# Attention vectors of the first graph layer computed beside the features, at the start of a two-layer graph kernel

## The chip, the cores and the metric

The kernel runs on one core of one Trainium2 chip. Its metric is the device time of one launch in microseconds (us). A core has five engines that work side by side, each through its own queue in order: TensorE (PE, matrix products; its weight loads are shown apart as PEld), VectorE (DVE), ScalarE (ACT), GpSimd (POOL), and SyncE (SP), which here only issues loads and stores. Matrix products land in PSUM[...]; everything else is in SBUF.

## The reference, cut to what matters

There are 64 graphs of 256 nodes with 512 features each, all in float32. Two layers follow each other, each with a residual and a layer norm.

```python
# layer 0: graph attention, 8 heads of 64 units
feats  = einsum('bnf,hfu->bhnu', x, W)
e_self = einsum('bhnu,hu->bhn', feats, a_self)      # one logit per node and head
e_neigh= einsum('bhnu,hu->bhn', feats, a_neigh)
dense  = leaky_relu(e_self[..., :, None] + e_neigh[..., None, :], 0.2)
att    = softmax(dense - 1e10 * (1 - adj))
out    = relu(einsum('bhij,bhju->bhiu', att, feats) + b)
x      = layernorm(x + out)
# layer 1: q, k, v of x; softmax(q k^T) * 0.33 + 0.33 * adj + 0.33 * exp(-adj); times v; W_out
x      = layernorm(x + layer1(x, nodemask, adj))
```

The logits need no features: `e_self = x @ (W_h a_self_h)`. The vector `W_h a_self_h`, 512 long for each head, is the "attention vector in x's space"; there are 16 of them, two per head.

## The kernel before, in words

Nodes are tiled in two tiles of 128 (`T = 2`), features in four blocks of 128 (`C = 4`), and heads in two groups of four (`HG = 4`). Graphs run one after the other, overlapped as a pipeline: while graph b is in layer 0, graph b-1 is in the projections of layer 1 and graph b-2 in its attention. The order of all work is written out by hand: each step is a call of `do(stage, graph, step)`, and `in_order` ties every instruction to the one before it on its engine. So the sequence of calls is the sequence of each engine's queue. The main loop (`attention0_beside_projections1`, `attention1_beside_projections0`) serves graphs 2 and later, with fast products of seven instead of eight block multiplications. Graphs 0 and 1 go through `start` and `second_beside_first` with plain products. Only `start` and the helpers that graphs 0 and 1 use are touched.

The steps in `start`, with their names in the profile:

- `xT_rows` (L524): x of graph 0 is turned by TensorE (tile `pt`) and copied to `xT` by ScalarE.
- `turned_weights` (L420, `pw`) turns the layer-0 weights `wf` by products with the identity; `attention_vectors` (L437, `pwa`) multiplies them with the attention coefficients (`a2`, made by GpSimd from `acol`), and VectorE copies the 16 vectors into `wa`.
- `features(t, g)` (L87 through `halved`, tile `pf`): the features of one node tile and one head group, four steps over the feature blocks, each as two half products of 64 columns of weights. `copied` (L673) adds the bias while it moves them from PSUM to `v`.
- `logits` (L663, `pl`): x times `wa`, graph 0 alone. In graph 1 `vectors_placed` (L448) has put the vectors beside the weights, so that the features come with their logits (66 columns per head instead of 64).
- `maxima` (L90 `pr`, L581 to L585): the logits are turned into rows, and the row maximum per head is taken; its second part spreads that maximum over the partitions by a product (L570, `pn`). `columns` (L612 to L620) makes the exponentials per node.
- `factors` (L606, `pg`): the exponentials of the rows, 8 rows, are spread over all partitions by a product with `sel`. 
- `aT`, `far`, `shared`: the adjacency, its exponentials, and the term it gives to layer 1.
- `weights` (L724, `pT`): VectorE makes the unnormalized attention of one head; `scaled` (L681) scales the features on ScalarE; `product` (L747, `av`) multiplies them; `norm0` divides, for graph 0 by VectorE (L768, L770), for the others by ScalarE (L778); `end`, `squares`, `norm` are residual and layer norm.
- `proj1 qk` and `values` (L87, `pq_p`, `pv_p`): layer 1.

`keep_busy` (L211) issues products of zeros that nothing reads, at five places in the start. Before `start`, the code issues the loads in the order of SP's queue: x, the mask, half of the layer-0 weights (the other half goes through ScalarE's queue), the attention coefficients, the bias, the adjacency, x of graph 1 and then all weights of layer 1 (`load_weights1`, L265).

PSUM is shared in two pools: tag `mm` has four tiles of one bank, tag `sc` two tiles of two banks.

Of the kernel before, what the change touches and what calls it, by code (L numbers as in the profile page):

```python
# [17 lines left out]
def kernel(  # L18
# [95 lines left out]

    X, XB, ADJB, MROW = {}, {}, {}, {}
# [33 lines left out]
    load_rows(0)  # L149
    mask_sb = io.tile([NB, N], U8, tag="mask", name="mask_sb", bufs=4)  # L150
    nc.sync.dma_start(mask_sb, nodemask)
    C2, F2 = C // 2, F // 2
# [11 lines left out]
    load_wf(nc.scalar, 0)  # L164
    load_wf(nc.sync, 1)

    acol = small.tile([P, 2, HG], FT, tag="acol", name="acol", bufs=1)
    for k, a in enumerate((a_self, a_neigh)):
        nc.sync.dma_start(acol[:, k, :], a.rearrange("(g r) u -> (r u) g", r=2))
# [3 lines left out]
    a2 = consts.tile([P, HG, 2, 2], FT, name="a2")  # L173
    nc.vector.memset(a2, 0.0)
# [5 lines left out]
    load_adj(0)  # L180
# [4 lines left out]
    wo_sb = consts.tile([P, 7, C2, F2], FT, name="wo_sb")  # L185
# [3 lines left out]
    for r in range(2):  # L189
        rows = slice(r * U, (r + 1) * U)  # L190
        nc.gpsimd.tensor_copy(a2[rows, :, r, :].rearrange("p g s -> p s g"), acol[rows])

    sel = work.tile([H, H + 1, P], FT, tag="rb", name="sel", bufs=1)
    nc.vector.memset(sel[:, H, :], 1.0)
# [13 lines left out]
    def keep_busy(dst, n):  # L208

        for _ in range(n):  # L210
            matmul(dst, idle, idle, start=True, stop=True)  # L211

    keep_busy(ps_tile([P, P], "pi"), 6)
    maskf = work.tile([NB, N], FT, tag="adjT", name="maskf", bufs=1)
    nc.vector.tensor_copy(maskf, mask_sb)
    pm = ps_tile([P, T, NB], "pm")
    for t in range(T):
        transpose(pm[:, t, :], maskf[:, t * P : (t + 1) * P])
    hide = consts.tile([P, T, NB], FT, name="hide")
    nc.vector.tensor_scalar(hide, pm, -1.0, HIDE, op0=ALU.add, op1=ALU.mult)  # L220
    m33 = consts.tile([P, T, NB], FT, name="m33")
    nc.vector.tensor_scalar_mul(m33, pm, L_BOTH)


    maskz = io.tile([NB, N], FT, tag="y", name="maskz", bufs=1)
    nc.vector.transpose(maskz, maskf)
# [188 lines left out]
    def turned_weights(g):  # L415

        pw = ps_tile([P, C, P], f"pw_{g}")
        for c in range(C):
            for r in range(2):
                matmul(  # L420
                    pw[r * U : (r + 1) * U, c, :],
                    wf[c // C2][g // 2][:, c % C2, 2 * (g % 2) + r, :U],
                    ident,
                    start=True,
                    stop=True,
                )
        tag = "both" if g < HG - 1 else "pT"
        wT = WA[g] = work.tile([P, C, P], FT, tag=tag, name=f"wT_{g}", bufs=4)
        nc.scalar.copy(wT, pw)
        in_order()  # L430

    def attention_vectors():

        pwa = ps_tile([P, C, HG, 4], "pwa")
        for g in range(HG):
            for c in range(C):
                matmul(pwa[:, c, g, :], WA[g][:, c, :], a2[:, g], start=True, stop=True)  # L437
        wa = WA["columns"] = work.tile([P, C, H, 2], FT, tag="hC", name="wa", bufs=1)
        nc.vector.tensor_copy(
            wa.rearrange("p c h s -> p (c h s)"), pwa.rearrange("p c g k -> p (c g k)")  # L440
        )
        in_order()

    def vectors_placed():

        for k in range(2):
            for g in range(2):
                nc.vector.tensor_copy(  # L448
                    wf[k][g][:, :, :, U:],
                    WA["columns"][:, k * C2 : (k + 1) * C2, g * HG : (g + 1) * HG],  # L450
                )
        in_order()
# [16 lines left out]
    def proj0(b):  # L469
# [14 lines left out]
        def far():  # L484
            AT[b] = work.tile([P, T, N], FT, tag="at", name=f"at_{b}", bufs=1)
            FAR[0] = work.tile([P, T, N], FT, tag="far", name=f"far_{b}", bufs=1)
            nc.scalar.activation(FAR[0], pa, AF.Exp, scale=-1.0)
            nc.scalar.activation(AT[b], pa, AF.Exp, bias=neg, scale=NEG)
            mrow = small.tile([P, N], FT, tag="mf", name=f"mf_{b}", bufs=1)
            nc.scalar.copy(mrow, MROW[b])  # L490
            FAR[1] = mrow
# [25 lines left out]
        def from_rows():  # L517
            for t in range(T):
                pt = ps_tile([P, C, P], f"pt_{b}_{t}")
                if t == 0:  # L520
                    keep_busy(pt[:, 0, :], 4)
# [40 lines left out]

        def maxima(part=None):

            if part == 1:
                pn = ps_tile([P, P], f"pn_{b}")
                if b == 0:
                    keep_busy(pn, 3)
                ROW["max"] = pn[:, :H]
                matmul(ROW["max"], sel[:, H, :], ROW["diag"], start=True, stop=True)  # L570
                return
            ps = ps_tile([P, 2, N], f"pr_{b}")
            if b == 0:
                keep_busy(ps[:, 0, :P], 3)
            ps = ps[:H]
            for s in range(2):
                for t in range(T):
                    transpose(ps[:, s, t * P : (t + 1) * P], V0[b][:, t, :, U + s])
            grow = small.tile([H, N + 1], FT, tag="grow", name=f"grow_{b}", bufs=1)
            nb = small.tile([H, 1], FT, tag="nb", name=f"nb_{b}", bufs=2)  # L580
            nc.vector.tensor_reduce(grow[:, N : N + 1], ps[:, 1, :], AX.X, ALU.max)  # L581
            nc.vector.tensor_scalar_mul(nb, grow[:, N : N + 1], -0.8)
            nc.scalar.activation(grow[:, :N], ps[:, 0, :], AF.Exp, bias=nb, scale=-0.8)
# [4 lines left out]
        def factors(part=None):  # L588
# [7 lines left out]
            h = HG if part == 1 else 0  # L596
            while h < (HG if part == 0 else H):
                n = 2 if b == 0 and h < HG else HG
                if n == 2:
                    pg = ps_tile([P, n, N], f"pg_{b}_{h}")  # L600
                else:
                    pg = psum.tile([P, n, N], FT, tag="sc", name=f"pg_{b}_{h}", bufs=2)
                if b == 0 and h == 0:
                    keep_busy(pg[:, 0, :P], 3)
                for k in range(n):
                    matmul(pg[:, k, :], sel[:, h + k, :], grow[:, :N], start=True, stop=True)  # L606
                    GB[b].append(pg[:, k, :])
                h += n

        def columns():  # L610
            nd = small.tile([P, T, H], FT, tag="nd", name=f"nd_{b}", bufs=2)
            nc.vector.tensor_sub(  # L612
                nd,
                V0[b][:, :, :, U + 1],
# [29 lines left out]
        def features(t, g):  # L644

            pf = PF[t, g] = ps_tile([P, HG, UX], f"pf_{b}_{t}_{g}")
            for c in range(C):
                halved(
                    pf[:, :, :cols],
                    xT[:, c, t * P : (t + 1) * P],  # L650
                    wf[c // C2][g][:, c % C2, :, :cols],
                    start=(c == 0),
# [3 lines left out]
        cols = U if b == 0 else UX  # L656

        def logits():

            pl = ps_tile([P, T, H, 2], f"pl_{b}")  # L660
            for t in range(T):
                for c in range(C):
                    matmul(  # L663
                        pl[:, t],
                        xT[:, c, t * P : (t + 1) * P],
                        WA["columns"][:, c],
                        start=(c == 0),
                        stop=(c == C - 1),
                    )
# [969 lines left out]
```

## Time and profile before

| | us |
|---|---|
| median of 3 runs | 2838.47 |
| lowest and highest | 2838.01, 2840.29 |
| the profiled execution | 2838.85 |
| its span | 2837.1 |
| first product of layer 1 (`pq_p`), graph 0, starts | 57.37 |
| first value product of layer 1 (`pv_p`), graph 0, starts | 77.46 |

The span is what the hardware profiler saw of one execution; the profiled execution's own time is 1.75 us longer. In the profile, a group line gives the source line, engine, operation, output and inputs with their shape (partitions x elements), the count, the busy time and the mean of one. A wait line gives who waited for whom, how long in sum, how often, and the longest. In a line of busy time by stage come the stretch, its length, then the busy time of each engine with its count, the TensorE clock that the chip granted (1.00 is full speed), the share of the DMA engines, and the rate. Products are pipelined, so the mean of one is longer than the pitch between two.

### The profile page before, as it was taken

Reading aid. Unit: us, or ns where it says so; the run is one execution under the profiler, and the core shown is the slowest. Engines: PE = TensorE matmul, PEld = TensorE weight load, DVE = VectorE, ACT = ScalarE, POOL = GpSimd, SP = SyncE. Lnnn points to the kernel's source line nnn. Section 1 sums busy time; section 2 is a strip of 40 time slices with the busy share of each in tenths; the row PEclk is TensorE's granted clock in tenths of the full one; section 3 lists DMA queues with packets and bytes.
Section 4 is the critical chain, followed back from the end, with each engine's and each line's share of the span. In section 5 each row is a group of like instructions: output and inputs, shape, how many; then the busy total and the mean of one; then the engine's idle time right before and its main releaser. Section 6 shows DMA issues by size and latency. Waiting matters only on the chain.

```text
span 2837.1 us, 93579 instructions
## 1 busy us (share of the span) xinstructions
PE 2813.9 (99%) x39172; PEld 2231.9 (79%) x39172; DVE 2556.9 (90%) x5135; ACT 1805.0 (64%) x5033; POOL 252.6 (9%) x528
## 2 busy tenths in 40 slices
PE   9999999999999999999999999999999999999998
PEld 7787787787787887887877888878778778788775
DVE  4999999999999999999999999999999999999984
ACT  3556666666666666666666666666666666666663
POOL 0000001000100100000010001001001000100011
PEclk9999999999999999999999999999999999999999
DMA  6445445554455454454454544554554544545532
GB/s 125 105 119 141 118 136 133 127 139 122 132 144 122 125 143 122 128 138 121 137 127 131 140 122 132 144 121 125 137 126 131 141 118 137 133 127 139 122 113 72
DMA packets 774508, 362.84 MB, mean 128 GB/s; under 512 B 690396, under 2 KB 692428, under 8 KB 758088
## 3 DMA queue, kind: packets, MB, share of 16 engines
q1 hardware_dynamic: 771976, 356.33, 48.5%
q8 instruction: 311, 5.10, 0.8%
q14 instruction: 109, 0.89, 0.1%
q10 hardware_dynamic: 2112, 0.52, 0.1%
HBM read 288.37 MB, written 68.13 MB: 126 GB/s over the span
## 4 chain that ended last, share of the span: by engine, by line
PE 97%; DVE 1%; DMA 1%; ACT 1%; issue 0%; POOL 0%; SPq 0%; DVEq 0%; POOLq 0%; ACTq 0%
PE pq_p L87 27%; PE po_p L87 14%; PE pf_p L87 13%; PE pv_p L87 13%; PE av L747 8%; PE pz L918 8%; PE av L1047 7%; PE pd L957 2%; PE pr L531 1%; PE pf L87 1%; PE po L87 0%; DMA x<-in_x_dram 0%; PE pg L606 0%; DMA mask_sb<-in_nodemask_dram 0%; PE pwa L437 0%
## 5 line engine op out<-in xcount | busy, mean ns | idle before, releaser
L87 PE MATMUL pq_p<-hC,wqk_sb 128*64 128x128 f32 x8192 | 469.7, 273 | 1.1 <-ACT qk L340 1.1
L87 PEld LDWEIGHTS pq_p<-hC,wqk_sb 128*64 128x64 f32 x8192 | 448.6, 137 | 2.3 <-ACT qk L340 1.5
L724 DVE SCALAR_TENSOR_TENSOR pT<-gb,ccol,at 128x256 f32<-128x256 f32 x992 | 403.4, 481 | 17.2 <-ACT ccol L619 17.2
L87 PE MATMUL pq_p<-hT,wqk_sb 128*64 128x128 f32 x6144 | 357.7, 273 | 0.4 <-ACT hT L880 0.4
L87 PEld LDWEIGHTS pq_p<-hT,wqk_sb 128*64 128x64 f32 x6144 | 342.0, 137 | 10.1 <-issue 0.7
L937 ACT ACTIVATE p<-pz,hide 128x512 f32<-128x512 f32 x638 | 333.3, 629 | 8.1 <-PE pz L918 1.0
L1028 DVE TENSOR_TENSOR p<-p,rb 128x1024 f32<-128x1024 f32 x252 | 299.2, 1208 | 3.6 <-DMA rb<-rs 3.6
L1037 DVE TENSOR_TENSOR p<-p,ct 128x1024 f32<-128x1024 f32 x252 | 299.5, 1209 | 0.2
L778 ACT ACTIVATE x<-av,rec 128x64 f32<-128x64 f32 x1008 | 220.3, 335 | 63.5 <-DVE rec L760 63.5
L747 PE MATMUL av<-v,pT 128*64 128x65 f32 x8192 | 253.1, 222 | 3.6 <-DVE pT L724 1.9
L681 ACT ACTIVATE v<-v 128x64 f32<-128x64 f32 x1024 | 251.3, 336 | 6.0 <-DVE v L673 6.0
L87 PE MATMUL pf_p<-wf_sb,xC 128*64 128x264 f32 x1984 | 253.6, 386 | 0.1
L747 PEld LDWEIGHTS av<-v,pT 128*64 128x64 f32 x8192 | 249.4, 138 | 5.3 <-issue 4.7
L87 PE MATMUL pv_p<-wv_sb,hC 128*64 128x256 f32 x2048 | 244.1, 379 | 2.5 <-ACT v L340 2.5
L340 ACT COPY qk<-pq_p 128x512 f32<-128x512 f32 x256 | 149.0, 582 | 153.4 <-PE pq_p L87 149.9
L1047 PE MATMUL av<-p,v 128*64 128x256 f32 x2016 | 240.0, 379 | 2.1 <-DVE p L1037 2.1
L918 PE MATMUL pz<-qk 64*128 64x256 f32 x2048 | 238.6, 383 | 0.0
L340 ACT COPY v<-pv_p 128x256 f32<-128x256 f32 x256 | 95.7, 374 | 221.4 <-PE pv_p L87 221.4
L87 PE MATMUL po_p<-wo_sb,oC 128*64 128x256 f32 x1984 | 235.2, 379 | 0.0
L394 POOL TENSOR_SCALAR rstd_l<-rstd_l 128x2 f32<-128x2 f32 (+1 forms) x130 | 96.2, 740 | 1532.5 <-ACT junk L383 1532.5
L918 PEld LDWEIGHTS pz<-qk 64*128 64x128 f32 x2048 | 192.6, 186 | 44.7 <-issue 24.6
L949 DVE SCALAR_TENSOR_TENSOR both<-p 128x512 f32<-128x512 f32 x256 | 172.4, 675 | 46.5 <-ACT p L937 46.2
(178 smaller groups left out, 4461.7 us busy)
## 6 DMA issues: line engine op xcount, KB each, us to landing
rb<-rs SPq DMA_DIRECT2D x63, 1024.0 KB
gb<-gs SPq DMA_DIRECT2D x62, 1028.0 KB
x<-in_x_dram SPq DMA_DIRECT2D x64, 512.0 KB
hs<-x SPq DMA_DIRECT2D x64, 512.0 KB
xb<-in_x_dram SPq DMA_DIRECT2D x252, 128.0 KB
y<-hs SPq DMA_DIRECT2D x63, 512.0 KB
out_dram<-y SPq DMA_DIRECT2D x63, 512.0 KB
hb<-hs SPq DMA_DIRECT2D x248, 128.0 KB
```

The lines of the kernel that those rows point to most:

```text
L87: matmul(dst[cols], lhsT[:, cols], rhs, **flags)
L340: nc.scalar.copy(out[COPIES[p]], dst)
L681: nc.scalar.activation(V0[b][:, t, h, :U], V0[b][:, t, h, :U], AF.Copy, scale=V0[b][:, t, h, U : U + 1],)
L724: nc.vector.scalar_tensor_tensor(pT[h][:, j, :], GB[b][h], CCOL[b][:, j, h : h + 1], AT[b][:, j, :], op0=ALU.max, op1=ALU.mult,)
L747: matmul(av[r * half : (r + 1) * half, k, :], pT[h][:, j, i : i + half], V0[b][:, j, h, :UA], start=(j == 0), stop=(j == T - 1),)
L778: nc.scalar.activation(X1[b][:, t, h * U : (h + 1) * U], av[:, k, :U], AF.Copy, scale=REC0[g][:, t, k : k + 1],)
L918: matmul(pz[r][:, j, :], QK[b][rows, g, 1, j * P : (j + 1) * P], QK[b][rows, g, 0, :], start=True, stop=True,)
L937: nc.scalar.activation(to, of, AF.Exp, bias=hide[:, j, b : b + 1], scale=U**-0.5,)
L949: nc.vector.scalar_tensor_tensor(both[g], p[:, :, 0, :], TINY, p[:, :, 1, :], op0=ALU.add, op1=ALU.add)
L1028: nc.vector.tensor_mul(p, p, REC[b][:, k : k + 2, g // 2, :] .unsqueeze(2) .to_broadcast([P, 2, T, N]),)
L1037: nc.vector.tensor_add(p, p, CT[b].unsqueeze(1).to_broadcast([P, 2, T, N]))
L1047: matmul(av[0][r * U : (r + 1) * U, g % 2, :], V1[b][:, j, 2 * g + r, :], PROBS[b][g][:, r, j, :], start=(j == 0), stop=(j == T - 1),)
```

## The change: what it does, and the diff

The attention vectors are no longer made by TensorE. Three one-row loads put the attention coefficients and the bias into one partition (`arow`, in space of `wo_sb` that is free then), ahead of everything else on SP's queue. A product with one row of ones spreads the coefficients over all partitions. VectorE (from PSUM) and GpSimd (from a copy that ScalarE makes) multiply them with the weights as they were loaded, and VectorE sums over the 64 units of each head.

The logits of graphs 0 and 1 come straight from x: once as rows (the vectors as weights, 40 columns of which 16 are used and the two kinds start at 0 and 32), once as columns for the neighbours' logits. The transposes of logits are gone, and graph 1's features have 64 columns per head again. The bias becomes the first product of each feature group, one row of ones times the bias row, and the scaling reads the features from PSUM, so that `copied` is gone. The mask's small steps go to ScalarE and behind the first features, graph 0's division goes to ScalarE, `vectors_placed` too. All fillers but four at the very start go. The layer-1 weights are loaded after the adjacency of graph 1, and the calls in `start` have a new order. The row broadcasts are all in two tiles of the `sc` pool.

```diff
+    wo_sb = consts.tile([P, 7, C2, F2], FT, name="wo_sb")
+    arow = wo_sb[0:1, 4:].rearrange("p k c f -> p k (c f)")
+    for k, a in enumerate((a_self, a_neigh, b0)):
+        nc.sync.dma_start(arow[:, k, :], a.rearrange("h u -> (h u)").unsqueeze(0))
+    X[0] = io.tile([P, T, F], FT, tag="hb", name="x_0", bufs=1)
+    for t in range(T):
+        nc.sync.dma_start(X[0][:, t, :], x[0, t * P : (t + 1) * P, :])
...
+    def masks(step):
+        if step == 0:
...
+            nc.scalar.copy(maskf, mask_sb)
+            nc.vector.transpose(maskz, maskf)
...
+        else:
+            pm = MASK.pop("pm")
+            nc.scalar.activation(hide, pm, AF.Copy, bias=-HIDE, scale=HIDE)
+            nc.scalar.mul(m33, pm, L_BOTH)
...
-    def turned_weights(g):
...
+    def attention_vectors(g):
+        if g == 0:
+            WA["psum"] = psum.tile([P, 2, 2, HG, U], FT, tag="sc", name="pa_bc", bufs=2)
+            WA["sbuf"] = io.tile([P, 2, 2, HG, U], FT, tag="x1", name="a_bc", bufs=1)
+            WA["columns"] = work.tile([P, C, 2, B], FT, tag="hC", name="wa", bufs=1)
+            nc.vector.memset(WA["columns"], 0.0)
+            for _ in range(4):
+                matmul(WA["psum"][:, 0, 0, :2], idle, idle, start=True, stop=True)
+        for k in range(2):
...
+            matmul(
+                WA["psum"][:, g, k].rearrange("p h u -> p (h u)"),
+                sel[0:1, H, :],
+                arow[:, k, cols],
...
+        nc.scalar.copy(WA["sbuf"][:, g], WA["psum"][:, g])
...
+    def logit_weights(g, c, step):
+        if step == 0:
...
+            engine, src = (nc.gpsimd, "sbuf") if c % 2 or g and c else (nc.vector, "psum")
+            engine.tensor_mul(
+                prod,
+                wf[c // C2][g][:, c % C2, :, :U].unsqueeze(1).to_broadcast([P, 2, HG, U]),
+                WA[src][:, g],
+            )
+        else:
+            nc.vector.tensor_reduce(
+                WA["columns"][:, c, :, g * HG : (g + 1) * HG], WA.pop((g, c)), AX.X, ALU.add
+            )
...
+        def logits():
+            pl = ps_tile([P, 2, N], f"pl_{b}")
+            for c in range(C):
+                matmul(
+                    pl[: B + H, 0],
+                    WA["columns"][:, c].rearrange("p s k -> p (s k)")[:, : B + H],
+                    xT[:, c],
...
+            near = pl[:, 1, : T * H].rearrange("p (t h) -> p t h", h=H)
+            for t in range(T):
+                for c in range(C):
+                    matmul(
+                        near[:, t],
+                        xT[:, c, t * P : (t + 1) * P],
+                        WA["columns"][:, c, 1, :H],
...
+        def features(t, g, c=None):
+            if c is None or c == 0:
+                PF[t, g] = ps_tile([P, HG, U], f"pf_{b}_{t}_{g}")
                 halved(
+                    PF[t, g],
+                    sel[0:1, H, :],
+                    arow[:, 2, g * HG * U : (g + 1) * HG * U],
+                    start=True,
+                    stop=False,
+                )
...
         def scaled(h):
             for t in range(T):
...
+                v = V0[b][:, t, h]
+                src = v[:, :U] if b > 1 else PF[t, h // HG][:, h % HG]
+                nc.scalar.activation(v[:, :U], src, AF.Copy, scale=v[:, U : U + 1])
```

The new order in `start`, up to the first product of layer 1:

```diff
+        attention_vectors(0)
+        attention_vectors(1)
+        for step in ((0, 0, 0), (0, 1, 0), (0, 3, 0), (0, 0, 1), (0, 2, 0), (0, 1, 1), (0, 2, 1), (0, 3, 1),
+                     (1, 1, 0), (1, 2, 0), (1, 0, 0), (1, 0, 1), (1, 1, 1), (1, 3, 0), (1, 2, 1), (1, 3, 1)):
+            logit_weights(*step)
         do("proj0", 0, "xT_rows")
+        # features of graph 0, group 0: for c in range(C), for t in range(T)
+        masks(0)
+        masks(1)
         do("proj0", 0, "logits")
+        # features (0, 1), blocks 0 and 1
         do("proj0", 0, "maxima")
         do("proj0", 0, "aT")
+        do("proj0", 0, "far", 0)
         load_adj(1)
+        combine_weights1 = load_weights1()
         do("proj0", 0, "maxima", 1)
+        # features (0, 1), blocks 2 and 3
         do("proj0", 0, "columns")
+        # factors 0, factors 1, features (1, 1)
+        # for h in 0..3: scaled, weights; then far 1; products (0, 0), (0, 1) of graph 0
         do("turned", 1, "xT")
         load(2)
+        do("attend0", 0, "rec0", 0)
+        # scaled h 4..7; norm0 (0, 0), (0, 1); weights 4, 5
+        do("proj0", 1, "logits")
         vectors_placed()
+        # graph 1: maxima; graph 0: weights 6, 7
+        # graph 1: features (0, 0), (1, 0), maxima 1; graph 0: products (1, 0), (1, 1)
+        # graph 1: columns, aT, far 0, factors 0, with graph 0's shared 0 behind columns
+        # graph 0: rec0 1, norm0 (1, t), end, squares; graph 1: features (0, 1), (1, 1), factors 1, scaled 0..3
+        # graph 0: norm, from_rows 0 and 1, blocks; load_rows(1); graph 1: weights 0..3
         do("proj1", 0, "qk", "p1")
```

After that, `combine_weights1`, `hC` and the other products of q and k follow as before, with `shared 1` of graph 0 and `far 1` of graph 1 after the product p6, and heads 4 to 7 of graph 1 after p7. The comments in this second part stand for the calls they name.

## The prediction

> **What bounds the kernel now.** I read the page first (shares, then the slices), then the waits of TensorE, then the busy time by stage, and last the groups by form of the first 77.5 us.
>
> ```profile
> PE 2813.9 (99%) x39172; PEld 2231.9 (79%) x39172; DVE 2556.9 (90%) x5135; ACT 1805.0 (64%) x5033; POOL 252.6 (9%) x528
> ```
>
> TensorE is busy 99% of the span, so only TensorE work, its waits or its clock can move the end. Of its named waits in the whole span, 16 us in sum, some 40% lie in the first 58 us; the two largest there:
>
> ```profile
> PE pm L90 <- DVE maskf L215: 2.6, 1, 2.6
> ...
> PE av L747 <- DVE pT L724: 1.9, 1, 1.9
> ```
>
> The columns of the next view, busy time by stage, are TensorE busy, weight loads, VectorE, ScalarE, GpSimd, granted clock, DMA share, GB/s:
>
> ```profile
> 12.70:19.50 6.80, 6.80 (x87) 5.96 (x83) 0.00 (x0) 2.27 (x4) 0.00 (x0) 1.00 0.67 102
> 19.50:29.70 10.20, 9.88 (x47) 8.36 (x48) 2.06 (x7) 0.46 (x1) 0.00 (x0) 0.50 1.35 225
> 29.70:36.60 6.90, 6.90 (x42) 5.26 (x40) 3.38 (x10) 3.67 (x13) 0.00 (x0) 0.99 1.03 153
> 36.60:40.00 3.40, 3.40 (x18) 1.96 (x16) 0.70 (x3) 0.00 (x0) 0.00 (x0) 0.50 0.00 0
> ...
> 57.40:77.50 20.10, 20.10 (x368) 18.72 (x370) 18.44 (x35) 8.36 (x27) 0.00 (x0) 1.00 0.40 104
> 77.50:2837.00 2759.50, 2743.02 (x38360) 2171.54 (x38354) 2516.66 (x5030) 1781.44 (x4970) 248.28 (x512) 1.00 0.49 128
> ```
>
> "Busy" hides something: in 19.5 to 29.7 and 36.6 to 40 us TensorE ran at half clock. Before 12.7 us there is no clock record and the 1.00 shown is empty; the durations say half clock there too: a 128x128 transpose of x took 421 ns at 8.8 to 10.3 us and 272 ns at 55.5. After 77.5 us (first value product of graph 0, 77.46) TensorE is full and that code is unchanged. So the change is worth what it moves that point.
>
> [...] the half-clock stretches are 10.24 and 3.41 us, three windows and one. [...] The window 33.2 to 36.6 was full of the row broadcasts pg (8 rows of weights) and the clock fell; 16.1 to 19.5 held 0.9 us of features and then pwa (4 columns) and it fell; 43.4 to 46.8 held 1.5 us of dense products and it stayed. So products with few rows or few columns count as idle, and about 1.2 to 1.5 us dense per window is the limit.
>
> **The change, part by part.** Prices are from these groups (busy us, mean ns):
>
> ```profile
> L606 PE MATMUL pg<-grow,sel 8*128 8x256 f32 x32 | 7.7, 384 | 0.0
> L437 PE MATMUL pwa<-a,wT 128*128 128x4 f32 x32 | 4.7, 284 | 0.0
> L420 PE MATMUL pw<-ident,wf_sb 128*64 128x128 f32 x48 | 4.2, 332 | 0.0
> L663 PE MATMUL pl<-wa,xT 128*128 128x16 f32 x16 | 3.6, 375 | 0.3 <-DVE wa L439 0.3
> ```
>
> An fp32 matmul is two such instructions. By their pitch in order of time: pg 3.65 us for 8 matmuls, 0.456 each; pwa 4.66 for 16, 0.29; a feature step (two halves, 256 columns) 1.73/4 = 0.43; all double, or nearly, at half clock.
>
> Removed from TensorE: turning the weights (pw) 4.63, pwa 4.66, graph 0's logits 3.60 at half clock, row transposes 0.85 and 0.8, and fillers 1.47 + 0.87 + 0.86 = 3.2 (those ahead of 9 us filled waiting time). Added: row logits, 4 matmuls of 40x256 at 0.43 = 1.7, and column logits, 8 at 0.29 = 2.35, in both graphs, 8.1; eight one-row bias products at 0.43 = 3.5, less 0.2 for graph 1's narrower features. Net 17.7 - 11.4 = 6.3 us less.
>
> Moved off TensorE: the vectors. Eight products of 128x512 and eight reductions. VectorE's 128x512 product takes 0.69 us (the add into qk); the reduction is not shown at this size, 0.41 us for 256 elements, so 0.5 to 0.8, I take 0.65. GpSimd at 128x512 is in no row; its 128x128 select took 0.29[...].
>
> Landing: first, three one-row loads, 0.45 us of issue each, ahead of x on SP's queue: x starts at 2.2 instead of 0.73, and the first data came 1.35 us after the issue. x needs about 2.7 us of the DMA engines and goes ahead of the 256-byte runs of the weights, which finish near 10.7. One-row products for the broadcast: 4 at half clock, 3.3 to 6.7 us. Products from 7.2; GpSimd's five run 8.0 to 9.3, 9.8 (fourth block) to 11.1, 12.4, 13.7, 15.0; last reduction 15.7. TensorE meanwhile: transposes 6.7 to 8.4, ten feature steps 8.4 to 14.9 (half clock until about 12.7), masks 0.3. So the vectors cost TensorE 0.5 us; the cover is graph 0's first features.
>
> Then with full clock, in order: logits 4.1 to 19.8; three steps 1.3; the maximum waits for ScalarE and VectorE (0.4) and takes 0.4; two steps 0.86; pg 3.65 to 26.4; features 2.16; products 2.0; logits 4.1 to 34.6; features 4.3; maximum 0.4; products 2.0; pg 1.9; features 4.3; pg 1.9; turning h 1.05; copy 0.5: the first q/k product at 51.0 (before: 57.37, with 3.84 of pg still to come). From there seven products 12.55 (16.4 less those 3.84 in the trace), 1.4 lost (below) and 3.75 of av: the value product at 68.7 instead of 77.46. That is 8.8 us, with full clock.
>
> The 1.4: behind the add of tile 11 VectorE has wqk 1.22, graph 0's shared 1.55, four heads of weights 3.2, wqk 1.22, add 0.69, in all 8.6 with the add itself, and TensorE has four products, 7.2, before p3 needs the last add.
>
> New waits in the order of the queues: TensorE's logits on the last reduction (all later TensorE work stands behind, 0.5 us as above); VectorE's reciprocal of graph 0 on the first products, with two heads of weights behind it, and its row maximum of graph 1 on graph 1's logits, with two more heads behind. These heads are used by the second products at 39, and VectorE has done them by 37: 2 us of cover, beyond that TensorE waits.
>
> Edits at nothing: masks to ScalarE (needed late), normalization of graph 0 to ScalarE (16 x 0.22, while TensorE does logits and features), scaling straight from PSUM (holds four of the four small banks until columns; the next tile comes after that), vectors placed by ScalarE. The layer-1 weights' sixteen loads (15.2 us of issue, 15.5 to 30.7 now) go behind graph 1's adjacency, which waits for VectorE's turn at about 21: issue to 40, data to 42. Behind them on SP is x of graph 2, needed at 78. First user is VectorE at 46 or later: hidden by 4 us at least; a further delay beyond that would be paid one for one.
>
> **The clock.** Between 15 and 26.4 there are only 1.7 us of dense steps; the fillers that stood there are gone. pg of graph 0 (3.65 plus a bias) must empty a window: one at half clock, 1.7 us lost. The two logits groups (2.8 us of thin work each, 4.5 if 40 columns count as thin) empty one more between them, or two, by the window's phase. I take two windows, 3.4 us, less the 0.4 of the maximum's wait, which a slower TensorE swallows: 8.8 - 3.0 = 5.8. Against the profiled execution's 2838.85 that is 2833.0; the median is 0.4 lower: about 2832.6.
>
> **Rivals.** *The clock eats it*: three or four windows half clocked (logits 0, pg 0, logits 1, pg 1). For: 40 columns and one row may count as idle, and no filler is left. Against: the before has four such windows too. Gain 8.8 - 5.2 to 6.8 = 2 to 3.6: about 2835.5. *The clock holds* (0 or 1 window): gain 7 to 9, about 2830.5. For: graph 1's features come in two blocks of 4.3 between thin groups. *GpSimd late*, the other side: five products in series, so each 0.1 us more on one moves the logits by 0.5. Lost are 5.8 us of forecast when the series is 5.8 longer, at 2.5 us a product; at 3 us, with a window emptied by the wait, 2842. For: never run here at this size[...].
>
> **How the numbers follow.** Forecast (two windows, 2831 to 2834.5) 0.50; clock eats it 0.22; clock holds 0.18; GpSimd late 0.10. Faster by over 0.2% means under 2832.8, the least a measurement of this kernel can tell from none: 0.30 of the forecast's half, all of "holds" and little else, 0.49. Slower by over 0.2% (above 2844.1) 0.06, the rest of "late" and all else 0.45. The range runs from 2828.5 (clock held, 10 us) to 2839.5 (GpSimd at 2.6 us).
>
> **What would show it.** Right: wa's last reduction by 16 us; the first q/k product at 52 to 57; the value product at 70 to 75; two half-clock stretches of one window between 19 and 45. Wrong: TensorE waiting for a reduction over 1 us; a clock at 0.50 for over 10 us; a wait for wqk's load; a wait in graph 0's first products for pT.

## The result, and the profile after

The kernel with the change takes 2844.22 us (median of 14 runs, 2838.32 to 2847.14), the kernel before on the same chip 2839.23 us (14 runs, 2836.55 to 2841.23): a ratio of 1.0017, 95% interval 1.0009 to 1.0026. So it is 5 us slower where 5.8 us of gain were forecast, outside the range of 2828.5 to 2839.5. The profiled execution took 2843.23 us, its span 2841.4.

The page's busy shares don't say why. TensorE has 62 instructions fewer and is busy 9.2 us longer:

```profile
PE 2823.1 (99%) x39110; PEld 2241.4 (79%) x39110; DVE 2559.0 (90%) x5125; ACT 1807.5 (64%) x5054; POOL 254.3 (9%) x531
```

The waits of TensorE up to 300 us. The two of before (2.6 for the mask, 1.9 for the attention of graph 0) are gone, and no new one is over 1.2 us:

```profile
PE pa_bc L420 <- DVE rowmask L177: 1.2, 1, 1.2
PE pq_p L87 <- ACT qk L337: 0.7, 1, 0.7
PE pa_bc L423 <- ACT a_bc L430: 0.7, 1, 0.7
```

Fewer instructions, fewer waits, more time: that leaves the clock, or new products that each take longer; the experiments decide between them. Busy time by stage (columns as before), cut at the edges of the clock records, the first of which is at 17.36 us (the 1.00 shown ahead of it is empty: a 128x128 transpose of x took 428 ns at 7.9 to 9.8 us and 279 in graph 1's, at 62.75):

```profile
17.40:24.20 6.80, 6.75 (x50) 4.14 (x46) 1.48 (x5) 1.33 (x4) 0.00 (x0) 1.00 0.16 23
24.20:37.80 13.60, 13.60 (x46) 8.31 (x47) 4.74 (x11) 3.41 (x14) 0.00 (x0) 0.50 0.83 161
37.80:44.70 6.90, 6.90 (x100) 5.22 (x98) 2.82 (x9) 4.16 (x20) 0.00 (x0) 0.99 1.04 192
44.70:51.50 6.80, 6.80 (x32) 2.99 (x28) 1.34 (x5) 0.01 (x1) 0.00 (x0) 0.50 0.44 69
51.50:64.08 12.58, 12.34 (x133) 8.40 (x131) 8.96 (x20) 7.97 (x27) 2.33 (x8) 1.00 0.13 42
64.08:81.70 17.62, 16.45 (x352) 15.96 (x354) 13.00 (x25) 5.44 (x16) 0.00 (x0) 1.00 0.48 114
81.70:2740.00 2658.30, 2657.22 (x37328) 2122.36 (x37326) 2458.86 (x4928) 1734.87 (x4860) 233.76 (x485) 1.00 0.50 130
```

A window is 3.41 us here: every stretch of the clock record but the last is a whole number of them (6.83 is two, 13.65 four). That a window's work goes with the clock of the next is the prediction's reading, and the window shares below bear it out. The half-clock stretches are four windows and two, where before had three and one. The first value product of layer 1 starts at 81.70 instead of 77.52 us, 4.2 later (77.46, given above for the kernel before, is the start of its weight load), and the span is 4.3 longer: in these two executions the whole loss lies ahead of that product. In order of time, what TensorE did around the late rise of the clock (17.36) and its first fall (24.18):

```profile
9.82 1.12 PE L87 MATMUL pf<-wo_sb,sel 1*64 1x256 f32 x4
10.87 1.12 PE L87 MATMUL pf<-wf_sb,xT 128*64 128x256 f32 x4
11.92 1.12 PE L87 MATMUL pf<-wo_sb,sel 1*64 1x256 f32 x4
12.97 5.39 PE L87 MATMUL pf<-wf_sb,xT 128*64 128x256 f32 x28
...
20.41 1.95 PE L585 MATMUL pl<-wa,xT 128*128 128x8 f32 x16
22.29 0.65 PE L87 MATMUL pf<-wo_sb,sel 1*64 1x256 f32 x4
22.87 1.08 PE L87 MATMUL pf<-wf,xT 128*64 128x256 f32 x8
...
26.29 7.19 PE L622 MATMUL pg<-grow,sel 8*128 8x256 f32 x16
```

The same 16 instructions of the row broadcasts `pg`, 7.19 us here, took about half in the kernel before:

```profile
32.68 3.72 PE L606 MATMUL pg<-grow,sel 8*128 8x256 f32 x16
```

And the groups by form that took the place of `pw`, `pwa` and graph 0's 16-column `pl` (busy us, mean ns, up to 82 us), first TensorE, then GpSimd:

```profile
L622 PE MATMUL pg<-grow,sel 8*128 8x256 f32 x32 | 11.2, 513 | 0.0
...
L87 PE MATMUL pf<-wo_sb,sel 1*64 1x256 f32 x32 | 7.1, 528 | 0.0
...
L585 PE MATMUL pl<-wa,xT 128*128 128x8 f32 x32 | 3.9, 257 | 0.0
L575 PE MATMUL pl<-xT,wa 128*40 128x256 f32 x16 | 3.8, 381 | 0.0
```

```profile
L440 POOL TENSOR_TENSOR prod<-wf_sb,a_bc 128x512 f32<-128x512 f32 x4 | 4.7, 1178 | 4.7 <-ACT a_bc L430 4.7
L440 POOL TENSOR_TENSOR prod<-wf,a_bc 128x512 f32<-128x512 f32 x1 | 1.2, 1187 | 1.9 <-DVE wa L446 1.9
```

GpSimd's product takes 1.18 us where the forecast has 1.3, the author's estimate that no trace of the kernel before shows, and the last reduction ends at 15.5 us (forecast 15.7). The bias line (`pf<-wo_sb,sel`) has one row of weights (1*64): 32 instructions, 7.1 us of busy time.

### The profile page after: what moved, and what is told of

The parts are those of the page before. It is cut to its first block, busy times and chain, and to the rows that moved or that the text cites. A ratio compares the mean times of both kernels' runs of the same rounds, so it can differ in the third digit from the quotient of the medians.

```text
span 2841.4 us, 93467 instructions
## 1 busy us (share of the span) xinstructions
PE 2823.1 (99%) x39110; PEld 2241.4 (79%) x39110; DVE 2559.0 (90%) x5125; ACT 1807.5 (64%) x5054; POOL 254.3 (9%) x531
## 4 chain that ended last, share of the span: by engine, by line
PE 98%; DVE 1%; ACT 1%; issue 0%; POOL 0%; POOLq 0%; DVEq 0%; ACTq 0%
PE pq_p L87 27%; PE po_p L87 14%; PE pf_p L87 14%; PE pv_p L87 13%; PE av L748 8%; PE pz L909 8%; PE av L1038 7%; PE pd L948 2%; PE pf L87 1%; PE pr L539 1%; PE po L87 0%; PE pg L622 0%; DVE p L1019 0%; PE pa_bc L423 0%; PE pl L585 0%
## 5 line engine op out<-in xcount | busy, mean ns | idle before, releaser
L688 ACT ACTIVATE v<-v 128x64 f32<-128x64 f32 x992 | 243.0, 336 | 0.0
```

What stands on the lines that cost most here:

```text
L688: nc.scalar.activation(v[:, :U], src, AF.Copy, scale=v[:, U : U + 1])
```

## The experiments

Two words are used from here on. A product is *full height* when its weights have all 128 rows, and *thin* when they have few rows (1 or 8) or when it streams few columns (4 to 16).

**The theory**: the time is the clock, and the bias products (one row) and the row broadcasts (8 rows) are what empties its windows. **The rivals**: the new products simply cost more time; or what was lost is the fillers that the change removed. The lever: a product over all 128 rows, of which all but the real ones are zero, gives the same sums and, as the runs below show for `pg` (16 instructions in 3.72 us over 8 rows and over 128), takes as long, but is full height.

In brief; each ratio is to the kernel before, run again beside it. "Half" are the half-clock windows between the first clock record and the first value product. They and the value product are those of one profiled execution, the medians those of 5 to 21:

| kernel | half | value product, us | median, us | ratio (95%) |
|---|---|---|---|---|
| before | 4 | 77.5 | 2839.23 | |
| the change | 6 | 81.7 | 2844.22 | 1.0017 (1.0009 to 1.0026) |
| both over 128 rows | 0 | 69.1 | 2831.28 | 0.9972 (0.9961 to 0.9984) |
| only `pg` over 128 | 3 | 75.8 | 2837.59 | 0.9994 (0.9986 to 1.0002) |
| only bias over 128 | 1 | 70.9 | 2833.59 | 0.9981 (0.9974 to 0.9988) |
| twelve fillers | 2 | 78.7 | 2849.55 | 1.0038 (1.0024 to 1.0051) |
| both over 32 | 5 | 80.0 | 2843.22 | 1.0016 (1.0009 to 1.0022) |
| both over 64 | 5 | 80.4 | 2842.59 | 1.0011 (1.0004 to 1.0017) |
| both over 128, no bias | 2 | 69.2 | 2828.48 | 0.9967 (0.9954 to 0.9979) |
| all one-row work over 128 | 0 | 65.0 | 2828.04 | 0.9962 (0.9950 to 0.9975) |
| before, `pg` over 128, late start | 3 | 82.5 | 2842.78 | 1.0018 (1.0011 to 1.0025) |
| before, no later fillers | 5 | 77.0 | 2839.04 | 1.0002 (0.9994 to 1.0010) |
| before, `pg` over 128 | 2 | 74.1 | 2837.07 | 0.9995 (0.9986 to 1.0003) |
| bias 128, `pg` 64 | 0 | 68.2 | 2832.22 | 0.9975 (0.9965 to 0.9985) |
| bias 128, `pg` 32 | 1 | 70.8 | 2833.78 | 0.9982 (0.9975 to 0.9989) |

### Bias and row broadcasts over all rows, together and one by one

The edit (the second and third kernel have one half of it each):

```diff
+    tall = work.tile([P, H + 1, P], FT, tag="rb", name="sel", bufs=1)
+    sel = tall[:H]
+    nc.gpsimd.memset(tall[:, :H], 0.0)
...
+    first = rowmask[:, 0, P // B : 2 * P // B].rearrange("p i b -> p (i b)")
+    nc.vector.memset(first, 0.0)
+    nc.vector.memset(first[0:1], 1.0)
...
+            wide = small.tile([P, N + 1], FT, tag="grow", name=f"grow_{b}", bufs=1)
+            nc.gpsimd.memset(wide[:, :N], 1.0)
+            grow = wide[:H]
...
-                        pg[:, k, :], sel[:, g * HG + k, :], grow[:, :N], start=True, stop=True
+                        pg[:, k, :], tall[:, g * HG + k, :], ROW["wide"][:, :N], start=True, stop=True
...
-                    sel[0:1, H, :],
-                    arow[:, 2, g * HG * U : (g + 1) * HG * U],
+                    first,
+                    brow[:, g * HG * U : (g + 1) * HG * U],
```

(`brow` is 128 rows of zeros with the bias in the first. With it, the bias is loaded behind x and no longer ahead of it. That brought no head start: VectorE writes more zeros first, and TensorE begins at 1.71 us, in the change at 1.17.)

> The changed kernel, with the row broadcasts (8 rows) and the bias products (1 row) made over all 128 rows: the added rows of weights are zero, so the result and the time of each product at a given clock are the same. Clock theory (products over few rows count as idle in the window that sets the TensorE clock, and six half-clock windows cost the forecast gain): the clock rises by 14 us, at most one half-clock window is left in 20 to 52 us, the first value product of layer 1 comes at about 70 to 73 us instead of 81.65, the time is 8 to 11 us under the changed kernel's, about 2834. Work theory (the 11.4 us of added TensorE work simply cost more than was removed, whatever the clock): the same time as the changed kernel, within 1.5 us, 2844.

> The changed kernel with only the row broadcasts over 128 rows. Clock theory: the half-clock stretch at 24 to 38 us shrinks to one or two windows, graph 1's stays; 4 to 6 us under the changed kernel, about 2839. Work theory: 2844.

> The changed kernel with only the bias products over 128 rows. Clock theory: the clock rises one window earlier at the start, graph 1 loses at most one window instead of two, the stretch over the row broadcasts stays; 3 to 6 us under the changed kernel, about 2840. Work theory: 2844.

Measured: 2831.28, 2837.59 and 2833.59 us. In the first, the stretch from the first clock record to the first q/k product, and two lines of its work in order of time:

```profile
14.30:51.50 37.20, 36.77 (x366) 26.38 (x362) 21.45 (x53) 16.91 (x64) 2.84 (x10) 1.00 0.74 137
```

```profile
20.72 0.65 PE L87 MATMUL pf<-wo_sb,rowmask 128*64 128x256 f32 x4
...
23.75 3.72 PE L633 MATMUL pg<-grow,sel 128*128 128x256 f32 x16
```

37.2 us without a break in the clock; `pg` is back at 3.72 us with 16 times the rows. The value product comes 12.6 us earlier than in the change, and the median is 12.9 lower than the change's, more than the 8 to 11 expected. So the clock explains the loss of 5 us and nearly all of the gain that didn't come. That the new products "cost too much" falls as the cause; they are all still there. About 0.7 of the 12.6 us isn't the clock: at full clock a group of bias products takes 0.43 to 0.48 us over 128 rows and took 0.58 over one. Alone, the bias over 128 rows lifts the clock 3.2 us earlier (14.2 instead of 17.4 us) and leaves one window, just behind `pg`:

```profile
23.72 3.72 PE L628 MATMUL pg<-grow,sel 8*128 8x256 f32 x16
...
27.88 1.93 PE L87 MATMUL pf<-wf,xT 128*64 128x256 f32 x8
29.58 1.85 PE L87 MATMUL pf<-wf_sb,xT 128*64 128x256 f32 x8
```

`pg` itself is fast (3.72 us), what follows takes nearly double (eight feature instructions 1.93 us, 1.03 in the first experiment): here the thin window was paid for by the next one. `pg` over 128 rows alone leaves three windows. So the one-row bias is the larger part; the two gains, 10.6 and 6.6 us by the medians, overlap and don't add. A part of the second may be chance: its clock rises at 15.91 instead of 17.36 us though nothing ahead of `pg` differs on TensorE, which is worth 0.7 us in the profiled execution.

### Fillers put back

```diff
+                if (b, t, g) in ((0, 0, 1), (1, 0, 0)):
+                    keep_busy(PF[t, g][:, :2], 3)
...
+                if (b, g) in ((0, 0), (0, 1)):
+                    keep_busy(pg[:, 0, :P], 3)
```

> The changed kernel with fillers back: three products of zeros each ahead of graph 0's second feature group, of each of its two row broadcasts, and of graph 1's first feature group (12 products, 3.5 us at full clock). Clock theory: they cost 3.5 us and save two to four half-clock windows of 1.7 us each: 0 to 4 us under the changed kernel, about 2842. Work theory: 3.5 us more, 2847.7.

Measured 2849.55 us, a miss: slower than the change, though the profiled execution has only two half-clock windows in the start and its value product 3.0 us earlier. Busy time at half clock in the start, and the last 100 us, of this kernel:

```profile
31.70:38.50 6.80, 6.80 (x61) 4.22 (x62) 1.85 (x3) 1.54 (x7) 0.00 (x0) 0.52 1.29 220
...
2740.00:2844.20 104.20, 87.86 (x998) 63.07 (x994) 57.04 (x98) 46.06 (x109) 10.38 (x25) 0.93 0.24 78
```

In the last 100 us, where the last graphs run out and TensorE waits, the clock was 0.93 on average; in the change it was 0.96. That code is the same in both. Over the whole run the mean clock is 0.995 to 0.996 in all five executions, no better than the change's 0.994 to 0.997. So the fillers' own 3.4 us came on top of a clock that was not better in sum. As a cure they fall; since they do take the windows in the start from six to two, their loss is not excluded as a part of the cause. At an equal mean clock of 0.996 this kernel is 4.4 us above the change (2848.2 against 2843.8). Where the profiled execution lost its lead can be read: at 2771.8 us it is still 4.0 us ahead of the change, and the last 72 us cost it 6.8, among them one wait of TensorE for VectorE's `both`, 2.6 us long, where the change has none. Why its end had two half-clock windows more than the change's is not settled.

### How many rows count: 32 and 64

The edit is that of the first experiment with `tall[:32]`, `first[:32]` and so on, then with 64.

> As the version with both kinds of products over all 128 rows, but over 32 rows. If the clock counts a product by its rows (the clock theory as I hold it), 32 of 128 is little more than 8 and the half-clock windows are back: first value product at 77 to 82 us, time 2840 to 2845. If it counts any product of 32 rows or more as work, it stays near the version over all rows, 69 us and 2831. The work theory, which fell with that version, would have no difference between the three.

> The same over 64 rows. Counting by rows: half of the work counts, so one or two half-clock windows, first value product at 70 to 75 us, 2832 to 2837. Counting any product of 32 rows or more: 69 us, 2831.

Measured 2843.22 and 2842.59 us, little better than the change; the second is a miss. Of 64 rows:

```profile
26.77 7.19 PE L633 MATMUL pg<-grow,sel 64*128 64x256 f32 x16
```

At half clock 64 rows did not lift the clock, though two whole windows (27.76 to 34.58 us) were full of 64-row products. But with 64 rows a window from 51.65 to 55.07 us held the clock with only 30% of its time in full-height work and the rest in `pg` and bias of 64 rows, where windows of the other kernels with 28 to 33% of it and thin work for the rest had fallen. That spoke for the share (64 rows count half), with a limit that is harder to reach at half clock. The last two runs below test it.

### Without the bias, and the version that beats both

The first experiment without its eight bias products (the bias of layer 0 is not added for graphs 0 and 1); and the first experiment with everything of one row over 128 rows, the broadcasts of the attention coefficients too, in a tile of its own for each head group:

```diff
-            WA["psum"] = psum.tile([P, 2, 2, HG, U], FT, tag="sc", name="pa_bc", bufs=2)
+        pa_bc = WA["psum", g] = psum.tile([P, 2, HG, U], FT, tag="sc", name=f"pa_bc_{g}", bufs=2)
...
-            for _ in range(4):
+            for _ in range(5):
...
-                sel[0:1, H, :],
+                first,
```

> The version over all 128 rows with the eight bias products left out (the bias of layer 0 is not added for graphs 0 and 1). At full clock these cost 8 x 0.43 = 3.5 us: first value product at 65.5 to 67.5 us instead of 69.1 (some of it may go into waits of VectorE and for the weights' vectors), time about 2828.5. If their price lay in the clock alone: no change, 69 us, 2831.

> The version over all 128 rows, with the broadcast of the attention coefficients over 128 rows too, and in a PSUM tile of its own for each head group, so that VectorE's first product doesn't wait for ScalarE's second copy. Clock theory: the clock rises one or two windows earlier, before 11.5 us, the first features end at 14 to 15 us instead of 16.7, the last reduction is done at 13 to 14.5: first value product at 66 to 68 us, 2829. If the start is bound by the arrival of the weights: no change, 69 us, 2831.

Measured 2828.48 and 2828.04 us. Leaving the bias out saves 2.8 us by the medians, though the ratios' intervals overlap. Its six runs are of two kinds: four at a mean clock of 0.999 take 2827.8 us on average, 3.6 less than the first experiment at that clock (2831.4), as priced, and two at 0.997 take 2832.8. The profiled execution is one of these two, so its value product, 69.2, missed the 65.5 to 67.5 expected. In it the full-height bias is missed: the window 17.75 to 21.16 us, with 40% of its time in such work, let the clock fall.

```profile
17.75:21.16 3.41, 3.24 (x26) 2.35 (x24) 1.11 (x4) 0.43 (x1) 0.00 (x0) 1.00 0.26 31
21.16:27.99 6.83, 6.37 (x19) 4.46 (x20) 0.78 (x5) 3.86 (x15) 0.00 (x0) 0.50 0.42 79
```

The other beats both kernels: 10.4 us under the kernel before, with the value product at 65.0, earlier than expected. Its clock is full from 6.82 us on, up to the first q/k product and beyond:

```profile
4.00 3.29 PE L433 MATMUL pa_bc<-wo_sb,rowmask 128*128 128x256 f32 x8
7.13 1.04 PE L90 MATMUL pt<-ident,x 128*128 128x128 f32 x8
```

```profile
7.06:47.30 40.24, 39.86 (x392) 28.58 (x389) 26.01 (x61) 18.70 (x68) 8.22 (x15) 1.00 0.75 143
```

The 0.7 us that TensorE had waited for ScalarE's copy between the two broadcasts is gone too (the eight instructions run on from 4.00 us without a gap), now that the copy no longer shares a tile with them. The two edits were made together; what each is worth was not measured.

### The same edit, and the fillers, in the kernel before

> The kernel before, with one edit: its row broadcasts pg run over all 128 rows, of which 120 of the weights are zero. If the rule (few rows count as idle) carries over: no stretch at 0.50 at 36.6 to 40.0 us, the pg of graph 0 still at full clock, the first value product at 75.4 to 76.2 instead of 77.46, the median 1.2 to 2 us under the kernel before (2836.5 to 2837.2, ratio 0.9993 to 0.9996). If rows have nothing to do with it: the stretch stays and the ratio is 1.0000.

> The kernel before without the nine zero products ahead of pr, pn and pg of graph 0, which took 3.2 us. If they count as work and hold the clock: the window from 26.3 no longer lifts it, TensorE stays at 0.50 from 19.5 until past pg, and the first value product comes at 77.5 to 82 in spite of 3.2 us less work; the median is 0 to 4 us above the kernel before. If they bought nothing: the value product at 74.3 and the median 2 to 3 us below.

> The kernel before with row broadcasts over all 128 rows, as in the run before this one, but the zeros are written by VectorE ahead of the mask's copy, not by GpSimd behind its wait for the attention coefficients, so that TensorE's first products are not 6.7 us late. If few rows count as idle here too: no stretch at 0.50 after pg of graph 0, first value product at 75.4 to 76.4 (77.46 in the kernel before), median 0.5 to 2 us under the kernel before, the rest up to the windows of the last 100 us. If the 1.7 us that the previous run won back between pg and the first av came from its late start and not from the rows: the stretch is back and the ratio is 1.0000.

In the first of the three the zeros were put in a bad place: they, 0.95 us of GpSimd's time, stood behind GpSimd's copy of the attention coefficients, which waits for their load. VectorE's writes to the same tile waited, and the mask's copy behind them:

```profile
13.25 0.44 PE L90 MATMUL pm<-ident,maskf 64*128 64x64 f32 x2 [9.28 <-DVE maskf L217]
```

TensorE started 6.7 us late, and the kernel is 4.7 us slower. Even so the stretch behind `pg` was gone: the first `av` is 4.93 us later than before's (46.45 against 41.52), so 1.8 of the 6.7 were won back there. With the zeros written by VectorE in time:

```profile
22.20:29.10 6.90, 6.90 (x32) 4.34 (x31) 1.83 (x6) 0.47 (x1) 0.00 (x0) 0.51 1.22 217
29.10:54.00 24.90, 22.19 (x272) 17.66 (x270) 17.21 (x51) 9.95 (x30) 3.62 (x9) 1.00 0.49 89
```

Two windows instead of four, the value product 3.4 us earlier (74.1, ahead of the 75.4 to 76.4 expected; the windows lay better ahead of `pg` as well), and the median 1.0 us lower, with an interval that takes in no change. In the profiled execution 1.8 us are lost again in the last 45 us. The mechanism carries over; its worth in time is at the limit of what these runs tell.

Without the nine later fillers the kernel before has one half-clock window more, and the value product comes at 77.0 us: 3.2 us of work saved, all but 0.5 lost again. The median doesn't move (1.0002). The forecast of 77.5 to 82 was nearly right: they bought about what they cost.

### What a window counts

Every window up to 66 us of thirteen kernels was then read in this way: the time of each product, times its rows over 128; products that stream 16 columns or fewer are left out; the sum divided by 3.41 us. The clock of the next window follows from it with one limit for each state. At full clock the lowest share that held was 0.41, the highest that fell 0.40; at half clock the lowest that rose was 0.86, the highest that did not 0.85. Half clock does about half the work in the same time (`pg` 7.19 us for 3.72), so the two limits are nearly one: 0.40 to 0.41 of the work that a window holds at full clock, and half of 0.85 to 0.86, that is 0.42 to 0.43; some 1.4 us of it. They don't meet exactly, and each rests on two windows. This was read off the traces, so it was tried on two new kernels, the first experiment with `pg` over 64 and over 32 rows:

> The bias over 128 rows, so the clock rises at 14.2 us as in the first experiment, and the row broadcasts pg over 64 rows, at full clock when they begin near 23.7. Share rule (a product counts by its share of 128 rows; a window at full clock holds with 41% or more): the worst window is pg alone, 50 to 56%, so the clock stays at 1.00, pg of graph 0 takes 3.7 us, first value product at 69.0 to 69.5, median 0 to 1 us from the first experiment's (2830.5 to 2832.5). Rule of nothing (64 rows count as idle): one window at 0.50 near 27.8 to 31.2, value product at 70.9, as with 8 rows.

> The same with pg over 32 rows. Share rule: the window 24.4 to 27.8 holds 13% dense work and 87% of pg at a quarter, 35% in sum, under 41%: one window at 0.50 near 27.8 to 31.2, value product at 70.6 to 71.0, median 2832.5 to 2835. If the clock stays at 1.00 here too, 32 rows count more than their share (or the windows lie so that pg is cut in two, which their edges would show).

Both came as the share rule said, each in the one window that could decide. With 64 rows, the window that holds 0.38 us of full height and 3.04 us of `pg` (11% and half of 89%: 56%), and the one after it:

```profile
22.29:25.71 3.42, 3.42 (x20) 2.66 (x15) 0.92 (x3) 2.80 (x12) 0.00 (x0) 1.00 0.50 79
25.71:29.12 3.41, 3.41 (x46) 2.32 (x45) 3.41 (x7) 0.37 (x2) 0.31 (x1) 1.00 0.75 160
```

With 32 rows, the same mix (11% and a quarter of 89%: 33%), and the one after it:

```profile
24.23:27.64 3.41, 3.41 (x19) 2.63 (x19) 1.90 (x5) 1.84 (x7) 0.24 (x1) 1.00 0.41 69
27.64:31.05 3.41, 3.41 (x20) 1.95 (x18) 2.47 (x5) 0.00 (x0) 0.07 (x1) 0.50 0.99 211
```

The medians are 2832.22 and 2833.78 us, as expected. The value product of the first, 68.2, is 0.8 us earlier than expected; its clock rose 2.2 us earlier than in the first experiment (12.05 for 14.24), though the code ahead of it is the same, and 2.2 us at full instead of half clock are worth 1.1.

How close the rule comes can be worked out from the windows. With these limits, a product over 64 rows counts 0.32 to 0.54 of one at full height, over 32 rows 0.12 to 0.34, over 8 rows at most 0.21. That rows count by their share lies within this; that they count exactly so is not shown.

## Why the prediction was wrong

The step that failed is the clock term, "I take two windows, 3.4 us": six windows and a late first rise took 12.5 us. The sum can be closed from the profile of the change. The forecast put the graph 0 logits at 15.7 and the first q/k product at 51.0 us with full clock: 35.3 us. They came at 18.56 and 64.08: 45.5 us, and six half-clock windows lose 6 x 1.7 = 10.2 of these. 35.3 is left, as forecast.

- **The work at full clock** was right in sum, in part by luck: a group of bias products took 0.58 us for 0.43, the column logits 1.9 for 2.35. From the first q/k to the value product 17.62 us (forecast 17.7); in the first experiment, where the clock holds, the two come at 51.50 and 69.1 (forecast 51.0 and 68.7). Nearly all of the 8.8 us were there to be had: in that experiment the value product comes 8.4 us earlier than before, and the median is 7.6 us lower.
- **GpSimd and VectorE**: right in size. 1.18 us a product for 1.3, an estimate that no trace of before had shown, reductions 0.62 to 0.69 us for 0.65; GpSimd's five took 1.17 to 1.19 us each, also those beside VectorE's products and reductions. That the last one came at 15.5 for 15.7 is in part luck: GpSimd began 2.1 us earlier than forecast (5.95 for 8.0), VectorE 1.4 later (8.64 for 7.2). The rival "GpSimd late" falls.
- **Hidden edits**: right. No wait of TensorE for the layer-1 weights, the masks, the placed vectors or the heads of weights shows.
- **Landing and first features**: 1.4 us late. The four broadcast products took 1.04 us each, 0.86 was assumed, and 0.7 us went into the wait for ScalarE's copy.
- **The clock** is the step that failed, in two places. "Half clock until about 12.7" was 17.36: in the window 10.53 to 13.94, two bias products took 1.4 us and features 2.0, so 59%, and it didn't lift. So 4.7 us more ran at half clock, which costs 2.3; with the 1.4 above, less the 0.5 us that TensorE was to wait for the last reduction, graph 0's logits should be 3.2 us late, and were 2.9. "I take two windows" was six: after the fall at 24.18 (1.08 us at full height, 32%), a window with 56% and two of thin work alone did not lift it, and after the one at 44.66 a window with 70% and a bias product did not. The prediction's own sign of being wrong, half clock for over 10 us, came: 13.65 us from 24.18 on.
- **The limit** of 1.2 to 1.5 us dense per window was nearly right, but only for holding full clock (1.4); the windows it was read from say no more than that 0.9 fell and 1.5 held. That a window of half clock needed as much work here to end it, 2.9 of its 3.4 us, was left out: each thin stretch was priced at one window. It cost one where full-height work filled the next window (the bias over 128 rows alone), and two or four where it didn't (the change, from 44.66 and from 24.18 us). And the bias products, priced at 3.5 us of TensorE, were left out of what empties a window, but for the one beside `pg`; only the rival names them ("one row may count as idle").

So 8.8 - 2.9 - 10.2 = -4.3 us at the value product, where 4.2 was measured. The nearest rival was "the clock eats it", with the right mechanism and half its size. Against it stood the argument that the kernel before "has four such windows too"; it has, and without its nine later fillers it had five. That its transposes, 128 rows high, kept the stretches short as well follows from the window shares alone.

The spread of the runs goes with the mean clock too. Over the 14 runs of the change the mean granted clock goes from 0.994 to 0.997, and the time with it: 2846.4 us in the run at 0.994, 2845.2 in the mean of six at 0.995, 2843.8 at 0.996 (five), 2839.9 at 0.997 (two). With 64 rows the 21 runs fall into two groups, 16 at 0.995 and 0.996 (2844.0 and 2842.5 in the mean) and five at 0.997 to 0.999 (2834.3 to 2836.6). The first records come at 12.05 us in one and 14.24 in another kernel with the same start, 2.2 us apart. Which runs fall on which side may be a matter of where the windows lie; with one trace of each kernel this is not shown.

## What to carry to other kernels

Before moving work between engines in a stretch where TensorE has mixed work, write down for each 3.4 us window how much of it is full-height work, rows over 128 times time. In these runs the next window ran at half speed when this was under 1.4 us, and it took 2.9 us in one window to come back. Products with few rows (a bias as a one-row product, a broadcast of a row) were dear in clock; padding them with zero rows made none of them slower (`pg` 3.72 us with 8 rows and with 128, a bias group 0.58 with one and 0.43 to 0.48 with 128) and was worth 12.9 us. Where the windows will lie was not known beforehand (2.2 us apart in two kernels with the same start), so leave some room. A padded tile needs its zeros written where no queue waits for a load (in the kernel before that cost TensorE 6.7 us).

## What the runs showed of the hardware that was not expected

- Rows count in the clock's window, about by their share, zeros among them, in these traces: in a window with 11% of full-height work and the rest `pg`, 64 rows held the clock (56%) and 32 rows let it fall (33%), with no other edit between the two kernels.
- Products that stream 4 or 8 columns counted as next to nothing (at most 0.12 and 0.01 of their time by the same working; for 16 columns it says only at most 0.43). Products with few columns of weights but 256 streamed counted: the row logits, with 40 columns of weights, at 0.87 or more. In the last kernel of the table, the window from 17.40 to 20.81 us had 7% of bias, 38% of row logits and 55% of column logits (8 streamed), and held.
- The limit was nearly the same work in both states (0.40 to 0.41 of a window at full clock, 0.42 to 0.43 at half), so the clock was much harder to lift (86% of a window) than to hold (41%).
- A one-row bias product was slower than one of 128 rows in its place: a bias group of four instructions took 0.58 us from start to start, at full clock, over one row, 0.57 to 0.58 over 32 and 64 rows, and 0.43 to 0.48 over 128. The row broadcasts show no such difference (`pg` 3.72 us over 8, 32, 64 and 128 rows); the cause was not sought.
